# A two-layer graph attention kernel: scores issued in one run, the opening and the last row regrouped, and one product for q, k and v in odd groups

## The chip, the cores and the metric

The kernel runs on one core of one Trainium2 chip. The metric is device time in microseconds, the median of several runs. Everything is fp32, apart from the adjacency mask (bytes).

## The reference

The input is 128 graphs of 128 nodes with 512 features each, and a boolean adjacency mask per graph. Two layers follow each other. Each computes attention between the nodes of a graph, masked by the adjacency, projects the result back to 512 features, adds its own input, and normalises the rows.

```python
# layer 0: 4 heads of 64; layer 1: 8 heads of 64
q, k, v = x @ Wq, x @ Wk, x @ Wv
sim = where(adj, q @ k.T * 64**-0.5, -finfo.max)
x = layernorm(x + softmax(sim) @ v @ Wo + bo)
h = layernorm(x) * gamma + beta
q, k, v = split(h @ w_qkv.T)
scores = where(adj | eye, q @ k.T * 64**-0.5, -1e9)
x = layernorm(x + softmax(scores) @ v @ w_out.T + b_out)
```

## The kernel before

Two graphs make one group; there are 64 groups (0 to 63). The work is software-pipelined over groups, with the order of every engine's instructions written out by hand: there is no scheduler. `opening()` handles the first groups, `step(s)` runs for s = 2 to 63, then come `closing_a`, `closing_b` (twice) and `last`. In step s the kernel computes

- layer 0's q, k, v of group s (`product_0`), its scores and softmax for group s - 1 (part 0), and its attention output and projection for group s - 2 (`attend(s, 0)`, `out_product(0, s - 2, ...)`);
- layer 1's q, k, v of group s - 3 (`qk`, `v`), its scores and softmax for group s - 4 (parts 1 and 2, one graph each), and its attention output and projection for group s - 5 (`attend(s, 1, 2)`, `out_product(1, s - 5, ...)`).

Every large product is a 2x2 block product in seven partial products, numbered 1 to 7. The sums of inputs that they need are made on GpSimd (`sums`, `out_sums`), the sums of weights once in the opening (`weight_sums...`). Partial products accumulate in PSUM banks: "a" and "f" (and "a0" and "f0") are single banks, and "mm" is a ring of four. Partial products 1, 5 and 6 are copied out by ScalarE (tiles `e`, `ev`, `eqk`), 2, 3 and 7 are added to such a copy by VectorE, and 4 is copied by ScalarE.

`scores(s, part)` multiplies q by k of 64-row heads, `masked` moves the scores under the mask into the tile `sm` (VectorE, L585), `maxima` takes negated row maxima (VectorE, L591), `exps` are ScalarE's, `normalised` multiplies by the reciprocal sum on GpSimd (L609), `blocks` turns the probabilities by 32x32 transposes and a round trip through DRAM (`blocks_direct` turns them on TensorE instead, L651), and `attend` multiplies them by v. Part 0's and part 2's scores take two banks each of the ring; part 1's take "a0" and "f0". `attend` of part 0 writes to "a", of part 1 to "f", of part 2 to the ring.

Layer 1's q and k of a group take a round trip through DRAM as well: `taken_tokens` writes them out, `kq_arrive` (on SP's queue) fetches them into `KQ`, and `q_in_order` (ScalarE, L426) makes from them the tiles `qo` (one for each graph), which `scores` reads as the stationary operand. `norms` (ScalarE, L746) are put on the list `later` and issued by `flush()`. `addend` (GpSimd, L701) adds the bias to the rows, and `with_self` (VectorE, L564) adds the diagonal to the mask of layer 1.

The tile `qkv0` has four slots of 128 columns per graph and head pair: even groups use slots 1 to 3 (q, k, v), odd groups slots 0 to 2. So v of two groups can be alive while q and k share slots. In the odd groups the kernel before keeps q in slot 1, k in slot 2 and v in slot 0, so that a partial product is issued as two matmul shapes, 256 columns (q, k) and 128 columns (v), into one bank. Groups 0 to 2 (`PLAIN_0`) hold q and k features by tokens and are computed in pieces of 128 columns. An fp32 matmul appears in the trace as two records for each instruction.

The last group's projection is plain (`out_plain`): two halves of 256 columns for each graph, in one bank for each graph. `add_plain` adds a half to the rows and takes its statistics; `root_plain` and `norm_plain` finish a row.

Of the kernel before, what the change touches and what calls it, by code (L numbers as in the profile page):

```python
# [10 lines left out]
F32 = mybir.dt.float32  # L11
# [6 lines left out]
P = 128  # L18
# [9 lines left out]
def kernel(ctx: ExitStack, tc: tile.TileContext, x, adj, wq, wk, wv, wo, bo,  # L28
                            gamma, beta, w_qkv, w_out, b_out, out):
    nc = tc.nc  # L30
# [15 lines left out]
    ps_st = ctx.enter_context(tc.tile_pool(name="ps_st", bufs=1, space=PSUM))  # L46
# [97 lines left out]
    wo1 = const.tile([P, INNER[1] // P, E], F32, name="wo1")  # L144
# [50 lines left out]
    KH = KC // 2  # L195
# [33 lines left out]
    qkv0 = const.tile([P, G, 2, 4, P], F32, name="qkv0")  # L229
# [30 lines left out]

    PLAIN_0 = (0, 1, 2)

    def turn_qk0(g):

        if not 0 <= g < NG or g in PLAIN_0:
            return
        t = one.tile([P, 4, 2, 4, 32], F32, tag="turned", bufs=2, name=f"turnedqk_{g}")
        for i in range(2):
            nc.vector.transpose(t[:, :, i], qkv0.rearrange("p b h t (q j) -> p q t (b h) j", j=32)[:, :, 1 + i])
        SCR[0] = put(t.rearrange("p q t m j -> p q (t m j)"), f"scrqk_{g}")  # L270

    def arrive_qk0(g):
# [3 lines left out]

    def q0_in_order(g):
        if 0 <= g < NG and g not in PLAIN_0:
            nc.scalar.copy(qkv0.rearrange("p b h t (a j) -> p t (b h) a j", j=32)[:, 1],
                           RAW[0][:, :, 0].rearrange("p a m j -> p m a j"))  # L280

    def finish(g, half):
# [29 lines left out]
    def sums(l, g):  # L312
        if not 0 <= g < NG:
            return
        xs = XS[l, g] = one.tile([P, 4, KH, N], F32, tag=f"xs{l}", name=f"xs{l}_{g}")
        halves_sums(xs, XT[l, g].rearrange("p (h c) (b n) -> p b h c n", h=2, b=2))
# [10 lines left out]
    XS, ACC, EV = {}, {}, {}  # L327
# [119 lines left out]
    def product_0(g, *which, ts=(0, 1, 2)):  # L447

        if not 0 <= g < NG:
            return  # L450
        xT = XT[0, g].rearrange("p (h c) (b n) -> p b h c n", h=2, b=2)
        xs = XS[0, g]
        odd = g % 2
        for i in which:
            left = {1: xT[:, 0, 0], 2: xT[:, 0, 1], 3: xs[:, 3], 4: xT[:, 1, 1], 5: xs[:, 0],
                    6: xs[:, 1], 7: xs[:, 2]}[i]
            right = {1: w0[:, :KH, :, 0], 2: w0[:, KH:, :, 0], 3: w0[:, KH:, :, 1], 4: ws0[:, 2],
                     5: w0[:, :KH, :, 1], 6: ws0[:, 0], 7: ws0[:, 1]}[i]
            bank, first = INTO[i]
            first = first and ts in ((0, 1, 2), (1,))  # L460
            if first and bank == "c":
                ACC[0, bank] = mm_tile(f"c0_{g}")
            elif first:
                ACC[0, bank] = ps_st.tile([P, 512], F32, tag=f"{bank}0", name=f"{bank}0_{g}")
            acc = ACC[0, bank]
            parts = acc[:, :3 * P].rearrange("p (t n) -> p t n", n=P)
            if g in PLAIN_0:
                todo = [(parts[:, (t + odd) % 3], *((right[:, c, t], left[:, c]) if t < 2 else
                                                    (left[:, c], right[:, c, t])))
                        for t in ts for c in range(KH)]  # L470
            elif odd:
                todo = [(parts[:, lo:hi], left[:, c], right[:, c, t0:t1])
                        for lo, hi, t0, t1 in ((1, 3, 0, 2), (0, 1, 2, 3)) for c in range(KH)]
            else:
                todo = [(parts, left[:, c], right[:, c]) for c in range(KH)]
            for n, (o, lhsT, rhs) in enumerate(todo):
                nc.tensor.matmul(o, lhsT, rhs, start=first and n == 0, stop=n == len(todo) - 1,  # L477
                                 skip_group_check=True)
            if 2 not in ts:
                continue  # L480
            src = acc[:, :3 * P]

            def whole(b, h):
                return qkv0[:, b, h, 1 - odd:4 - odd].rearrange("p t n -> p (t n)")

            if i in (1, 5, 6):
                EV[0, i] = one.tile([P, 512], F32, tag=f"e{i}", name=f"e0_{i}_{g}")[:, :3 * P]
                nc.scalar.copy(EV[0, i], src)
            elif i == 4:
                nc.scalar.copy(whole(1, 0), src)  # L490
            else:
                b, h, e = {2: (0, 0, 1), 3: (0, 1, 6), 7: (1, 1, 5)}[i]
                nc.vector.tensor_add(whole(b, h), src, EV[0, e])


    def out_product(l, g, *which):
# [35 lines left out]
    def scores(s, *parts):  # L532

        made = {}
        for part in parts or PARTS:
            g = group_of(s, part)
            if g is None:
                continue
            if part == 1:
                ps = [ps_st.tile([P, 512], F32, tag=t, name=f"sc{part}_{g}_{t}") for t in ("a0", "f0")]  # L540
            else:
                ps = [mm_tile(f"sc{part}_{g}_{i}") for i in range(2)]
            ps = [x.rearrange("p (k n) -> p k n", n=N) for x in ps]
            if part == 0:
                for b in range(G):
                    for h in range(HEADS[0]):
                        r = slice((h % 2) * D, (h % 2 + 1) * D)
                        k_ = (qkv0[r, b, h // 2, 2].rearrange("p (a j) -> p a j", j=32) if g in PLAIN_0 else
                              RAW[0][r, :, 1, b * K0 + h // 2])
                        nc.tensor.matmul(ps[h % 2][:, b * K0 + h // 2, :].rearrange("p (a j) -> p a j", j=32),  # L550
                                         qkv0[r, b, h // 2, 1], k_, start=True, stop=True)
            else:
                b = part - 1
                for h in range(HEADS[1]):
                    r = slice((h % 2) * D, (h % 2 + 1) * D)
                    nc.tensor.matmul(ps[h % 2][:, h // 2, :].rearrange("p (a j) -> p a j", j=32),  # L556
                                     QO[g, b][r, h // 2], KQ[r, :, 0, b, h // 2], start=True, stop=True)
            made[part] = ps
        return made

    def with_self(g):

        if 0 <= g < NG:
            nc.vector.tensor_tensor(M[g], M[g], eye[:, None, :].to_broadcast([P, G, N]), op=ALU.max)  # L564
# [195 lines left out]
    def out_plain(g, b, *steps):  # L760

        n = E // 2
        if 0 in steps:
            ACC["op", b] = ps_st.tile([P, 512], F32, tag=("a0", "f0")[b], name=f"op_{b}")
        acc = ACC["op", b]
        for i in steps:
            h = slice(i * n, (i + 1) * n)
            for c in range(K1):
                nc.tensor.matmul(acc[:, h], AT[1, g][:, b, c], wo1[:, c, h], start=i == 0 and c == 0,
                                 stop=c == K1 - 1, skip_group_check=True)  # L770

    def add_plain(g, b, i):

        n = E // 2
        h = slice(i * n, (i + 1) * n)
        row = R[g][:, b, h]
        if i == 0:
            ST[b] = two.tile([P, 2, nc.vector.BN_STATS_DIM], F32, tag="st_last", name=f"st_last{b}")
        nc.vector.tensor_add(row, ACC["op", b][:, h], row)
        nc.vector.bn_stats(ST[b][:, i], row)  # L780

    def root_plain(b):
# [26 lines left out]
    def opening():  # L809
# [20 lines left out]
        made = scores(1)  # L830
# [16 lines left out]
        prepare(2)  # L847
        product_0(1, 4)
        transposed(2)
        sums(0, 2)  # L850

    def step(s):

        made = scores(s, 0)
        attend(s, 1)
        made.update(scores(s, 1, 2))
        if s > 3:
            sums(0, s)
            arrive(s - 3)
# [1 line left out]
        load_ahead(s + 1)  # L861
        load_rows(s - 1)
        masked(made, s, 0, 1, 2)
        attend(s, 0, 2)
        maxima(s, *((0,) if s == 4 else (0, 1)))
        if s == 3:
            turn(s - 3)
            arrive(s - 3)
        out_sums(0, s - 2)
        if s == 3:  # L870
            sums(0, s)
            with_self(s - 3)
        exps(s, 0, 0)
        product_0(s, 1)
        exps(s, 0, 1)
        out_product(0, s - 2, 1, 2, *(() if s == 2 else (5,)))
        maxima(s, *((1, 2) if s == 4 else (2,)))
        product_0(s, 2)
        if s == 2:
            out_product(0, s - 2, 5, 6)  # L880
        normalised(s, 0)
        out_product(0, s - 2, *(() if s == 2 else (6,)), 3)
        exps(s, 1, 0)
        stats(0, s - 2, 0)
        product_0(s, 6)
        exps(s, 1, 1)
        out_product(0, s - 2, 7)
        (blocks_direct if s == 2 else blocks)(s, 0)
        product_0(s, 5)
        out_product(0, s - 2, 4)  # L890
        normalised(s, 1)
        finish(s - 3, 0)
# [7 lines left out]
        blocks(s, 1)  # L900
        product_0(s, 3)
        if s == 3:
            weight_sums(w1qk, wsqk, 1)
        product_0(s, 4)
        transposed(s + 1)
# [36 lines left out]
        out_product(1, s - 5, 7, 3, 4)  # L942
        q0_in_order(s)
        q_in_order(s - 3)
        addend(0, s - 1)
        v(s - 3, 7)
        stats(1, s - 5, 0)
        v(s - 3, 3)
        stats(1, s - 5, 1)
        v(s - 3, 4)  # L950
        if s > 2:
            with_self(s - 2)
        if s == NG - 1:
            arrive(s - 2)
            addend(1, s - 4)
# [197 lines left out]
```

## Time and profile before

| what | value |
|---|---|
| median of 3 runs | 2761.13 us (2759.78 to 2761.82) |
| the profiled execution | 2759.77 us |
| its span, first to last instruction | 2758.0 us |
| mean granted TensorE clock | 0.999 |
| TensorE matmul busy | 2743.3 us, 15811 records |
| TensorE weight loads busy | 2032.5 us |
| VectorE busy | 2033.5 us |
| ScalarE busy | 1506.1 us |
| GpSimd busy | 1752.0 us |
| DMA moved | 562.73 MB, 204 GB/s in the mean |

In lines of the profile, PE is TensorE's matmul, PEld its weight load, DVE VectorE, ACT ScalarE, POOL GpSimd and SP the queue that issues the DMAs. A timeline line gives the start in us from the beginning of the span, the time in us, engine, line of the kernel and operation, what is written and read, the shape, and how many like records were merged; in brackets stands the engine's idle time before it, with what ended it. Ends of matmuls are modelled and overlap the next start, so distances between starts are the better measure.

### The profile page before, as it was taken

What the parts mean: (1) busy time and instruction counts of PE and PEld (TensorE: products, weight loads), DVE (VectorE), ACT (ScalarE), POOL (GpSimd) and SP (SyncE); (2) the same over time, 40 slices, a digit from 0 to 9 for tenths busy, and PEclk for the clock granted to TensorE, in tenths of its full rate; (3) what the DMA queues carried; (4) which work ended last, traced back from release to release, by engine and by line L of the source; (5) the groups of instructions that cost most, each with busy time, mean ns of one, the idle gap of its engine ahead of it and who ended that gap; (6) DMA issues with size and microseconds to landing.
All of it is one profiled execution on the core that took longest, in us unless ns stands there. A gap on an engine that the chain in (4) does not pass through costs nothing.

```text
span 2758.0 us, 49315 instructions
## 1 busy us (share of the span) xinstructions
PE 2743.3 (99%) x15811; PEld 2032.5 (74%) x15811; DVE 2033.5 (74%) x3671; ACT 1506.1 (55%) x4804; POOL 1752.0 (64%) x2311
## 2 busy tenths in 40 slices
PE   9999999999999999999999999999999999999998
PEld 8867767677776677776776767777767777677688
DVE  6777777777777777777777777777777777777765
ACT  3456465464564654645646546456465464564654
POOL 5565666666656666666566666665666666656664
PEclk9999999999999999999999999999999999999999
DMA  6567777777777777777777777777777777777652
GB/s 179 154 200 206 218 217 204 218 210 215 212 202 219 216 204 219 210 216 209 205 217 217 204 219 210 214 213 203 216 218 203 215 214 215 211 204 220 201 150 65
DMA packets 550290, 562.73 MB, mean 204 GB/s; under 512 B 55560, under 2 KB 468752, under 8 KB 550032
## 3 DMA queue, kind: packets, MB, share of 16 engines
q1 hardware_dynamic: 550032, 559.58, 71.5%
q8 instruction: 127, 2.08, 0.3%
q14 instruction: 131, 1.07, 0.1%
HBM read 300.95 MB, written 258.47 MB: 203 GB/s over the span
## 4 chain that ended last, share of the span: by engine, by line
PE 97%; DMA 1%; DVE 1%; issue 0%; SPq 0%; ACT 0%; POOL 0%; POOLq 0%; DVEq 0%; ACTq 0%
PE qka L361 16%; PE a L477 12%; PE oa L517 12%; PE va L361 8%; PE qkf L361 8%; PE av L679 7%; PE f L477 6%; PE of L517 6%; PE vf L361 4%; PE qkc L361 4%; PE oc L517 3%; PE c L477 3%; PE sc L550 2%; PE sc_a L556 2%; PE sc L556 2%; PE vc L361 2%
## 5 line engine op out<-in xcount | busy, mean ns | idle before, releaser
L600 ACT ACTIVATE sm<-sm,nmax 128x128 f32<-128x128 f32 x1536 | 594.8, 391 | 30.6 <-DVE nmax L591 27.9
L609 POOL TENSOR_TENSOR sm<-sm,rec 128x1024 f32<-128x1024 f32 x192 | 364.1, 1896 | 333.7 <-DVE rec L608 330.7
L701 POOL TENSOR_TENSOR r<-r,bias 128x1024 f32<-128x1024 f32 x128 | 301.5, 2356 | 130.9 <-ACT r L700 130.9
L521 DVE TENSOR_TENSOR r<-oa,r 128x256 f32<-128x256 f32 x508 | 211.1, 415 | 134.9 <-PE oa L517 129.4
L600 ACT ACTIVATION_READ_ACCUMULATOR sm<-sm,nmax 128x1 f32 x1536 | 291.4, 190 | 0.0
L371 ACT COPY ev<-va 128x256 f32<-128x256 f32 x128 | 47.6, 372 | 432.8 <-PE va L361 432.8
L627 DVE STREAM_TRANSPOSE turnedp<-sm 128x1024 f32<-128x1024 f32 x188 | 233.6, 1243 | 64.5 <-POOL sm L609 53.9
L720 POOL TENSOR_SCALAR ve<-mv 128x2 f32<-128x2 f32 x191 | 41.7, 218 | 371.4 <-DVE mv L713 360.9
L591 DVE TENSOR_REDUCE nmax<-sm 128x8 f32<-128x1024 f32 x192 | 226.6, 1206 | 0.3
L361 PE MATMUL qkf<-w,xs 128*128 128x512 f32 x472 | 221.8, 592 | 0.0
L361 PE MATMUL qka<-wsqk,xs 128*128 128x512 f32 x472 | 221.8, 592 | 0.0
L517 PE MATMUL of<-wo,so 128*128 128x256 f32 x760 | 205.9, 379 | 1.4 <-DVE r L521 1.0
L517 PE MATMUL oa<-wso,so 128*128 128x256 f32 x760 | 206.0, 380 | 0.4 <-DVE r L521 0.4
L324 POOL TENSOR_TENSOR xs<-xT 128x256 f32<-128x256 f32 x256 | 187.7, 733 | 22.4 <-DVE xT L118 18.6
L746 ACT ACTIVATE r<-r,shift,root 128x512 f32<-128x512 f32 x254 | 193.0, 809 | 2.5 <-POOL shift L735 2.5
L426 ACT ACTIVATE qo<-kq 128x512 f32<-128x512 f32 x118 | 67.9, 622 | 228.6 <-DMA kq<-scrkq 228.6
L324 POOL TENSOR_TENSOR so<-aT 128x256 f32<-128x256 f32 (+1 forms) x254 | 150.2, 591 | 52.1 <-ACT aT L682 44.6
L477 PE MATMUL f<-w,xs 128*128 128x128 f32 (+1 forms) x760 | 182.2, 376 | 0.2 <-DVE w L214 0.2
L477 PE MATMUL a<-ws,xs 128*128 128x128 f32 (+1 forms) x760 | 182.1, 375 | 0.0
L585 DVE COPY_PREDICATED sm<-m,sc 128x512 f32<-128x512 uint8 x256 | 172.4, 727 | 11.1 <-PE sc L550 2.2
L712 DVE BATCH_NORM_STATS2 st<-r 128x6 f32<-128x512 f32 x254 | 174.9, 689 | 2.3
L571 POOL MEMSET sm<- 128x1024 f32 x192 | 175.1, 952 | 1.4 <-DVE turnedp L627 1.4
(181 smaller groups left out, 6471.9 us busy)
## 6 DMA issues: line engine op xcount, KB each, us to landing
scrp<-turnedp SPq DMA_DIRECT2D x188, 512.0 KB, 3.6
pT<-scrp SPq DMA_DIRECT2D x752, 128.0 KB, 2.9
kq<-scrkq SPq DMA_DIRECT2D x236, 256.0 KB, 4.8
x<-in_x_dram SPq DMA_DIRECT2D x256, 128.0 KB, 4.0
r<-in_x_dram SPq DMA_DIRECT2D x64, 512.0 KB, 4.0
out_dram<-r SPq DMA_DIRECT2D x63, 512.0 KB, 3.6
scr<-turned SPq DMA_DIRECT2D x62, 512.0 KB, 6.7
kq<-scr SPq DMA_DIRECT2D x248, 128.0 KB, 2.8
```

The lines of the kernel that those rows point to most:

```text
L324: nc.gpsimd.tensor_tensor(o, a0, a1, op=op)
L361: nc.tensor.matmul(o, lhsT, rhs, start=first and m == 0, stop=m == len(todo) - 1, skip_group_check=True)
L477: nc.tensor.matmul(o, lhsT, rhs, start=first and n == 0, stop=n == len(todo) - 1, skip_group_check=True)
L517: nc.tensor.matmul(acc, left[:, c], right[:, c], start=first and c == 0, stop=c == hk - 1, skip_group_check=True)
L521: nc.vector.tensor_add(part, acc, part)
L591: nc.vector.tensor_reduce(NMAX[part], SM[part], AX.X, ALU.max, negate=True)
L600: nc.scalar.activation(sm[:, i, k, :], sm[:, i, k, :], AF.Exp, bias=nmax[:, i, k:k + 1], accum_out=total[:, i, k:k + 1])
L609: nc.gpsimd.tensor_tensor(SM[part], SM[part], rec[:, :, :, None].to_broadcast([P, 2, K1, N]), op=ALU.mult)
L627: nc.vector.transpose(t.rearrange("p q (h r) -> p q h r", r=32), SM.pop(part).rearrange("p i k (q r) -> p q (i k) r", r=32))
L679: nc.tensor.matmul(pm[i * D:(i + 1) * D, at, :].rearrange("p (a r) -> p a r", r=32), v, pT[:, :, i * K1 + at, :], start=True, stop=True)
L701: nc.gpsimd.tensor_tensor(R[g], R[g], (bias0, bias1)[l][:, None, :].to_broadcast([P, G, E]), op=ALU.add)
L746: nc.scalar.activation(R[g][:, b], R[g][:, b], AF.Identity, bias=shift[:, b:b + 1], scale=root[:, b:b + 1])
```

## The change

The change has four parts; `closing_a`, `closing_b` and the order of `last` keep as they are.

- `step` issues the scores of all three parts in one run, and then all three parts of `attend`, in the order 0, 1, 2. Before, part 1's `attend` stood between the scores of part 0 and those of parts 1 and 2.
- `product_0` of odd groups issues one matmul of 384 columns for each half of the contraction instead of one of 256 and one of 128. The bank then holds q, k, v in this order in all groups. For odd groups the evictions write the three runs backwards, so that v stays in slot 0, k in slot 1 and q in slot 2; `QK0` tells the readers where q and k are.
- In `opening` and steps 2 to 4: the input sums of group 2 move from the end of the opening into step 2, behind the output sums; part 0's exps move as a whole behind the first `product_0`; in step 4 part 2's maximum moves behind part 1's first exps; in step 2 `blocks_direct` moves behind one more product; in step 3 an `addend` moves ahead of a block of weight sums, and `with_self` of group 0 moves to the end of the step.
- `out_plain` puts each half into a bank of its own, four in all.

```diff
+    QK0 = ((1, 2), (2, 1))
...
-            nc.vector.transpose(t[:, :, i], qkv0.rearrange("p b h t (q j) -> p q t (b h) j", j=32)[:, :, 1 + i])
+            nc.vector.transpose(t[:, :, i], qkv0.rearrange("p b h t (q j) -> p q t (b h) j", j=32)[:, :, QK0[g % 2][i]])
...
-            nc.scalar.copy(qkv0.rearrange("p b h t (a j) -> p t (b h) a j", j=32)[:, 1],
+            nc.scalar.copy(qkv0.rearrange("p b h t (a j) -> p t (b h) a j", j=32)[:, QK0[g % 2][0]],
...
-                todo = [(parts[:, (t + odd) % 3], *((right[:, c, t], left[:, c]) if t < 2 else
+                todo = [(parts[:, t], *((right[:, c, t], left[:, c]) if t < 2 else
...
-            elif odd:
-                todo = [(parts[:, lo:hi], left[:, c], right[:, c, t0:t1])
-                        for lo, hi, t0, t1 in ((1, 3, 0, 2), (0, 1, 2, 3)) for c in range(KH)]
             else:
                 todo = [(parts, left[:, c], right[:, c]) for c in range(KH)]
...
             def whole(b, h):
-                return qkv0[:, b, h, 1 - odd:4 - odd].rearrange("p t n -> p (t n)")
+                return qkv0[:, b, h, 2::-1] if odd else qkv0[:, b, h, 1:4]
...
-                nc.scalar.copy(EV[0, i], src)
+                nc.scalar.copy(EV[0, i], acc[:, :3 * P])
             elif i == 4:
-                nc.scalar.copy(whole(1, 0), src)
+                nc.scalar.copy(whole(1, 0), parts)
             else:
                 b, h, e = {2: (0, 0, 1), 3: (0, 1, 6), 7: (1, 1, 5)}[i]
-                nc.vector.tensor_add(whole(b, h), src, EV[0, e])
+                nc.vector.tensor_add(whole(b, h), parts, EV[0, e].rearrange("p (t n) -> p t n", n=P))
...
+                        q_at, k_at = QK0[g % 2]
-                        k_ = (qkv0[r, b, h // 2, 2].rearrange("p (a j) -> p a j", j=32) if g in PLAIN_0 else
+                        k_ = (qkv0[r, b, h // 2, k_at].rearrange("p (a j) -> p a j", j=32) if g in PLAIN_0 else
                               RAW[0][r, :, 1, b * K0 + h // 2])
...
-                                         qkv0[r, b, h // 2, 1], k_, start=True, stop=True)
+                                         qkv0[r, b, h // 2, q_at], k_, start=True, stop=True)
...
     def out_plain(g, b, *steps):
         n = E // 2
-        if 0 in steps:
-            ACC["op", b] = ps_st.tile([P, 512], F32, tag=("a0", "f0")[b], name=f"op_{b}")
-        acc = ACC["op", b]
         for i in steps:
-            h = slice(i * n, (i + 1) * n)
+            acc = ACC["op", b, i] = ps_st.tile([P, 512], F32, tag=(("a0", "a"), ("f0", "f"))[b][i], name=f"op_{b}{i}")
             for c in range(K1):
-                nc.tensor.matmul(acc[:, h], AT[1, g][:, b, c], wo1[:, c, h], start=i == 0 and c == 0,
+                nc.tensor.matmul(acc[:, :n], AT[1, g][:, b, c], wo1[:, c, i * n:(i + 1) * n], start=c == 0,
                                  stop=c == K1 - 1, skip_group_check=True)
...
-        nc.vector.tensor_add(row, ACC["op", b][:, h], row)
+        nc.vector.tensor_add(row, ACC["op", b, i][:, :n], row)
...
         transposed(2)
-        sums(0, 2)
 
     def step(s):
-        made = scores(s, 0)
-        attend(s, 1)
-        made.update(scores(s, 1, 2))
+        made = scores(s)
...
-        attend(s, 0, 2)
+        attend(s)
         maxima(s, *((0,) if s == 4 else (0, 1)))
...
         out_sums(0, s - 2)
-        if s == 3:
+        if s in (2, 3):
             sums(0, s)
-            with_self(s - 3)
-        exps(s, 0, 0)
+        if s > 4:
+            exps(s, 0, 0)
         product_0(s, 1)
-        exps(s, 0, 1)
+        exps(s, 0, *((0, 1) if s < 5 else (1,)))
         out_product(0, s - 2, 1, 2, *(() if s == 2 else (5,)))
-        maxima(s, *((1, 2) if s == 4 else (2,)))
+        maxima(s, 1 if s == 4 else 2)
...
         exps(s, 1, 0)
+        if s == 4:
+            maxima(s, 2)
...
-        (blocks_direct if s == 2 else blocks)(s, 0)
+        if s > 2:
+            blocks(s, 0)
         product_0(s, 5)
+        if s == 2:
+            blocks_direct(s, 0)
...
         product_0(s, 3)
         if s == 3:
+            addend(0, s - 1)
             weight_sums(w1qk, wsqk, 1)
...
-        addend(0, s - 1)
+        if s != 3:
+            addend(0, s - 1)
...
-        if s > 2:
-            with_self(s - 2)
+        for g in {2: (), 3: (0, 1)}.get(s, (s - 2,)):
+            with_self(g)
```

More of the change, by code (lines that the diff above doesn't have):

```diff
@@ L480, in product_0 @@
                 continue
-            src = acc[:, :3 * P]
             def whole(b, h):
-                return qkv0[:, b, h, 1 - odd:4 - odd].rearrange("p t n -> p (t n)")
+                return qkv0[:, b, h, 2::-1] if odd else qkv0[:, b, h, 1:4]
             if i in (1, 5, 6):
                 EV[0, i] = one.tile([P, 512], F32, tag=f"e{i}", name=f"e0_{i}_{g}")[:, :3 * P]
-                nc.scalar.copy(EV[0, i], src)
+                nc.scalar.copy(EV[0, i], acc[:, :3 * P])
             elif i == 4:
-                nc.scalar.copy(whole(1, 0), src)
+                nc.scalar.copy(whole(1, 0), parts)
             else:
                 b, h, e = {2: (0, 0, 1), 3: (0, 1, 6), 7: (1, 1, 5)}[i]
-                nc.vector.tensor_add(whole(b, h), src, EV[0, e])
+                nc.vector.tensor_add(whole(b, h), parts, EV[0, e].rearrange("p (t n) -> p t n", n=P))
     def out_product(l, g, *which):
```

## The prediction

> **What bounds the kernel now.** I read the page first (busy shares, then the chain that ended last), then a window over the steady part, then TensorE's timeline of one step.
>
> ```profile
> PE 2743.3 (99%) x15811; PEld 2032.5 (74%) x15811; DVE 2033.5 (74%) x3671; ACT 1506.1 (55%) x4804; POOL 1752.0 (64%) x2311
> PE 97%; DMA 1%; DVE 1%; issue 0%; SPq 0%; ACT 0%; POOL 0%; POOLq 0%; DVEq 0%; ACTq 0%
> 130.00:2588.00 2458.00, 2458.00 (x13659) 1782.16 (x13656) 1831.57 (x3302) 1359.82 (x4345) 1578.72 (x2080) 1.00 0.75 212
> ```
>
> From 130 to 2588 us the matrix engine has no idle time, at a full clock. Only what shortens TensorE's own stream, or makes it wait, moves the end. A busy PE is not a PE at its peak, so I take the distance between **starts** in the timeline, not durations. One step (it starts at its first score matmul, L550) has a switch of matmul kind three times in its head:
>
> ```profile
> 1315.74 1.16 PE L550 MATMUL sc<-rawqk,qkv 64*128 64x128 f32 x16
> 1316.83 1.09 PE L679 MATMUL av<-pT,v 128*64 128x128 f32 x16
> 1317.86 0.37 PE L556 MATMUL sc_a<-kq,qo 64*128 64x128 f32 x1
> ...
> 1318.85 1.06 PE L556 MATMUL sc<-kq,qo 64*128 64x128 f32 x16
> 1319.84 1.09 PE L679 MATMUL av<-pT,qkv 128*64 128x128 f32 x16
> 1320.77 1.04 PE L679 MATMUL av<-pT,v 128*64 128x128 f32 x16
> 1321.74 1.57 PE L477 MATMUL a<-w,xT 128*128 128x256 f32 x8
> ```
>
> Step 4 has no attend of part 1 yet, so its three score groups already stand in one run:
>
> ```profile
> 92.35 1.16 PE L550 MATMUL sc<-rawqk,qkv 64*128 64x128 f32 x16
> ...
> 95.22 1.09 PE L679 MATMUL av<-pT,qkv 128*64 128x128 f32 x16
> 96.25 1.56 PE L477 MATMUL a<-w,xT 128*128 128x384 f32 x4
> ```
>
> And the products of layer 0, in an odd step (two shapes, 8 records) and in an even one (4 records):
>
> ```profile
> 1331.41 1.47 PE L477 MATMUL f<-w,xs 128*128 128x256 f32 x8
> 1332.72 1.47 PE L477 MATMUL a<-ws,xT 128*128 128x256 f32 x8
> ...
> 106.45 1.45 PE L477 MATMUL f<-w,xs 128*128 128x384 f32 x4
> 107.74 1.45 PE L477 MATMUL a<-ws,xT 128*128 128x384 f32 x4
> ```
>
> **What the Trainium skill says.** "TensorEngine Tiling (Array Packing)", Key Properties: changing the tiling mode, not just the tile, drains TensorE. The trace agrees: scores use 64 rows (64*128), attend 64 columns (128*64), products the whole array. Pairs of records follow each other every 0.112 us in a score run and every 0.109 us in an attend run; a pair at a switch takes 0.20 to 0.21 us and the next one is late again, while sc to sc_a and av to av cost nothing extra. "TensorE: Matmul & The Clock Gate", LDWEIGHTS (loading the stationary operand): a load costs columns/1.2, thus 107 ns for 128 columns (an estimate from the page). A 128x128 matmul record starts its successor 111 ns later, against 106.7 ns for 128 columns within wider records (322.5 for 384 minus 215.8 for 256): it lies at that floor. "SBUF — State Buffer", Who interferes with whom: VectorE and GpSimd share a port pair under an exclusive lock. The trace agrees in the opening: a VectorE weight sum (L214, at 81.09 us) took 2.57 us beside a GpSimd add, its like just before 0.42.
>
> **The change part by part.**
>
> 1. Scores in one run, steps 5 to 63 (59 steps). Before, head to first product: 1321.74 - 1315.74 = 6.00 us. After: scores in one run 95.22 - 92.35 = 2.87; then av, av, av. The two av runs that already follow each other take 1321.74 - 1319.84 = 1.90; another 8 pairs at 0.109 add 0.87. Sum 5.64 to 5.65. Saved 0.354 us (from the unrounded starts) x 59 = **-20.9 us**. No matmul is removed; one return to scores (0.20) and one more entry into attend (0.15) are.
>
> 2. Odd groups' q, k, v in one product. 31 odd groups (3 to 63), 7 products each. An odd product takes 1.307 to 1.310 us (four records at 215.8 and four at 111 ns), an even one 1.290. Over a step it is 0.13: odd steps last 42.49 us from scores to scores, even ones 42.35. 31 x 0.13 = **-4.0 us**. It removes 31 x 7 x 4 = 868 matmul records and as many weight loads. The evictions change only their order of writing (three runs of 128, backwards); no row of before shows a backward write. Forward they take 0.55 us on VectorE and 0.46 on ScalarE. If backward cost half more, three VectorE adds would add 0.8 us in a step in which VectorE is busy 1831.57/2458 = 75%; that hides in its 10 us of idle time, otherwise it would delay TensorE by at most that. I take 0. The changed index of the transposes and of ScalarE's q copy moves the same bytes.
>
> 3. A new wait. sc_a now starts about 1.0 us after the step's start instead of 2.1, and needs qo of half 0, which ScalarE makes when the kq DMAs land:
>
> ```profile
> 1315.24 1.15 ACT L426 ACTIVATE qo<-kq 128x512 f32<-128x512 f32 x2 [3.69 <-DMA kq<-scrkq]
> ```
>
> Half 0 is done at 1315.87, 0.13 after the step's start. Over the steps with such rows its median is 0.25 after the start, with a scatter of -0.6 to +2.02. In 8 (steps 7, 9, 17, 38, 44, 54, 61, 63) it comes later than 0.92, which leaves 0.08 for the semaphore; the excess sums to **+3.1 us**. Before, 2.1 us covered all: the waits of TensorE show this one once, 0.9 us, in the closing. Everything on TensorE queues behind sc_a: the second half's scores, the three attends, product 1. The kq DMAs are issued from SP after the qk products of the step before, whose distance to the step's end doesn't change, so I keep this distribution; half a microsecond of general delay makes 9.3. Bounds: +1 to +9.
>
> Part 1's eviction on ScalarE now stands behind the norms (done near +4.3 in the step) and lands near +5.6; the first to need its bank is the of matmul at +8. sc_a's banks come free at the last r add, 2.06 us before the step's start. VectorE gets its last scores earlier and is done with masking near +5.2 instead of 5.97, while the first product moves only to 5.65: no new wait. SP issues nothing for attend; its order is unchanged there.
>
> 4. Opening, steps 2 to 4. Waits of TensorE there, from starts against the record's own spacing: 0.53 and 0.98 (of at 43.91 and 45.95), 0.47 (pt at 48.70), 0.35 (of at 65.08), 0.60 (qka at 84.32), 0.55 (oa at 102.93), together 3.5 us.
>
> ```profile
> 45.95 0.67 PE L517 MATMUL of<-wo,so 128*128 128x256 f32 x2 [0.81 <-DVE r L521]
> 102.93 0.67 PE L517 MATMUL oa<-wso,so 128*128 128x256 f32 x2 [0.38 <-DVE r L521]
> ```
>
> Each edit meets one: sums(0, 2) go behind the out sums on POOL (so was ready 2 to 3 us late); the exps go behind ScalarE's e copy, on which a VectorE eviction and then the r adds waited; the transposes by TensorE go one product (1.3 us) later; with_self leaves the head of step 3; one maximum (1.2 us) leaves the queue ahead of r in step 4; the addend (2.5 us on POOL) moves away from weight sums, the 2.57 us one among them. It then lies beside transposes and other weight sums, and may delay qk there. No DMA moves. I take **-3.0**; bounds -3.5 and +1.
>
> 5. Last row. Four banks instead of two: VectorE's add of half 0 no longer waits for the whole row.
>
> ```profile
> 2751.11 0.42 DVE L779 TENSOR_TENSOR r<-op,r 128x256 f32<-128x256 f32 x1 [1.47 <-PE op L769]
> 2752.36 0.42 DVE L779 TENSOR_TENSOR r<-op,r 128x256 f32<-128x256 f32 x1
> ```
>
> Half 0 is then added near 2749.5, the first row's norm fits before 2751.1, and the last add starts at 2751.11 instead of 2752.36: **-1.25**; bounds 0 and -1.4. The two further banks were evicted before 2744.
>
> Sum: -20.9 - 4.0 + 3.1 - 3.0 - 1.25 = -26.0. The profiled execution took 2759.77 (span 2758.0 and 1.77 around it): 2733.7. The median of the runs, 2761.13, lies 1.36 higher, and I give the time against it: **2735.0**, 0.9% below. About 0.2%, 5.5 us, is what a measurement of this kernel can tell from no change.
>
> **Rivals.** (a) *The drain stays*: the cost belongs to each block's entry, not to the mode. Then part 1 gives nothing: 2735 + 21 = 2756, faster by 0.19%, no change. Against it stand the blocks of like kind that follow each other at full pace. Chance 0.02. (b) *qo becomes the bound*, the slower side: the kq round trip through DRAM ends later in every step, because the DMA queues (75% busy) or SP's order shift. Shifting the measured arrivals by 1.05 us makes the waits 28 us and eats all gains; at 1.5 us they are 52, and the time is 2735 + 49 = 2784. For it: ScalarE waits 3.7 us for this DMA per step, so nothing but the DMA sets it. Against: what feeds it is not moved. Chance 0.04. (c) *The opening gives nothing or a microsecond back, and late kq transfers come often*: 2735 + 4 + 6 = 2745, still faster. Chance 0.12, within the forecast's sign. The forecast proper has 0.82.
>
> The range adds the bounds: best -20.9 - 4.3 + 1 - 3.5 - 1.4 = -29, thus 2732, less 2 for scatter between runs; worst with +9 and no gain in the opening -17, 2744. I give 2730 to 2743. Faster 0.94, same 0.02, slower 0.04.
>
> **What would show it.** Right: 48 av records in one run after 48 score records, steps of 42.0 us, odd and even alike; no 128x128 or 128x256 form of layer 0's products in odd groups after 1; about 14943 matmul records; waits "sc_a from ACT qo" in some eight steps, 2 to 5 us in all; no wait for r at 45 and 103 us; the last VectorE chain about 1.2 us shorter. Wrong: sc_a waiting in most steps, VectorE evictions above 0.7 us in odd steps, odd steps still 0.13 longer, or TensorE waiting for masked scores ahead of product 1.

## The result, and the profile after

The changed kernel takes 2736.12 us (median of 4 runs, 2734.58 to 2737.01), beside 2760.73 for the kernel before (4 runs): a ratio of 0.991, with a 95% interval of 0.9893 to 0.9927. The forecast was 2735.0. The profiled execution took 2737.01 us, its span 2735.2: 22.8 less than the span of before.

From the page of the changed kernel, the busy line, and from a window over its steady part the row of busy times:

```profile
PE 2720.4 (99%) x14943; PEld 1933.5 (71%) x14943; DVE 2027.1 (74%) x3671; ACT 1503.3 (55%) x4804; POOL 1750.5 (64%) x2311
130.00:2567.00 2437.00, 2435.13 (x12818) 1687.42 (x12812) 1828.22 (x3300) 1356.93 (x4345) 1576.64 (x2080) 1.00 0.75 213
```

14943 matmul records are 868 fewer, as counted. TensorE still sets the end, but is no longer without a gap: 1.87 us of idle time have come into the window, where there was none.

TensorE's timeline of the head of step 32 in the changed kernel (columns: start, time, engine, line, operation, output and inputs, shape, count; layer 1's scores, between the first two rows, are left out):

```profile
1262.71 1.16 PE L548 MATMUL sc<-rawqk,qkv 64*128 64x128 f32 x16
...
1265.59 1.09 PE L677 MATMUL av<-pT,qkv 128*64 128x128 f32 x16
1266.51 1.92 PE L677 MATMUL av<-pT,v 128*64 128x128 f32 x32
1268.36 1.56 PE L476 MATMUL a<-w,xT 128*128 128x384 f32 x4
```

All 48 score records come first, then 48 av records, with no gap at a seam between blocks of like kind. The head of a step, from its first score to its first product, takes 1268.36 - 1262.71 = 5.65 us, where the kernel before took 6.00. The distance from one step's first score to the next's is 42.00 us in odd and even steps alike (before: 42.49 and 42.35).

Where the 22.8 us of the span went, from the starts of the steps in both profiles: the start of step 1 came 1.5 later (the weights' first DMAs landed later; in the twelve profiles of this study it lies anywhere from 22.1 to 23.9 us); step 1 to step 5 took 102.6 instead of 105.8 (-3.2; the two belong together, as the run with the opening's edits alone shows below, and make -1.7); the 58 steps from step 5 to step 63 took 2440.8 instead of 2460.4 (-19.6); step 63 47.2 instead of 48.3 (-1.1); from step 64's scores to the last matmul 115.2 instead of 114.4 (+0.8, of which 0.5 is a wait for ScalarE's xT that the profile of before does not have); the tail behind the last matmul 5.67 instead of 6.90 (-1.2). The profile of before fell on the fastest of its four runs and that of the changed kernel on the slowest of its four, so the spans differ by less than the medians (24.6).

The new wait is there too. The waits of TensorE, and step 26 in TensorE's and ScalarE's timelines:

```profile
PE sc_a L554 <- ACT qo L428: 1.9, 4, 0.9
1008.70 1.16 PE L548 MATMUL sc<-rawqk,qkv 64*128 64x128 f32 x16
1010.78 0.37 PE L554 MATMUL sc_a<-kq,qo 64*128 64x128 f32 x1 [0.92 <-ACT qo L428]
1010.10 1.15 ACT L428 ACTIVATE qo<-kq 128x512 f32<-128x512 f32 x2 [5.58 <-DMA kq<-scrkq]
```

ScalarE had been idle for 5.58 us until the kq DMAs landed; half 0 of qo (half of the 1.15) was done 2.03 us after the step's first score, and sc_a started 0.05 after that, at 2.08 instead of 1.0. The wait list counts 1.9 us in four gaps; measured on the starts, nine steps lost 4.3 in their heads. Steps 5 to 63 are 4.7 longer than their median in all: the other 0.4 lies almost wholly at the end of step 7, where the last partial product of layer 1's v waits for VectorE's copy of v.

### The profile page after: what moved, and what is told of

The parts are those of the page before. It is cut to its first block, busy times and chain, and to the rows that moved or that the text cites. A ratio compares the mean times of both kernels' runs of the same rounds, so it can differ in the third digit from the quotient of the medians.

```text
span 2735.2 us, 47645 instructions
## 1 busy us (share of the span) xinstructions
PE 2720.4 (99%) x14943; PEld 1933.5 (71%) x14943; DVE 2027.1 (74%) x3671; ACT 1503.3 (55%) x4804; POOL 1750.5 (64%) x2311
## 3 DMA queue, kind: packets, MB, share of 16 engines
q14 instruction: 130, 1.06, 0.1%
## 4 chain that ended last, share of the span: by engine, by line
PE 96%; DMA 2%; SPq 1%; ACT 0%; issue 0%; DVE 0%; POOL 0%; POOLq 0%; ACTq 0%; DVEq 0%
PE qka L363 16%; PE a L476 12%; PE oa L514 11%; PE qkf L363 8%; PE va L363 8%; PE av L677 6%; PE f L476 6%; PE of L514 6%; PE qkc L363 4%; PE vf L363 4%; PE c L476 3%; PE oc L514 3%; PE sc L548 2%; PE sc L554 2%; PE vc L363 2%; PE sc_a L554 2%
## 5 line engine op out<-in xcount | busy, mean ns | idle before, releaser
L476 PE MATMUL f<-w,xs 128*128 128x384 f32 (+1 forms) x512 | 181.1, 476 | 0.2 <-DVE w L214 0.2
L476 PE MATMUL a<-ws,xs 128*128 128x384 f32 (+1 forms) x512 | 181.0, 476 | 0.0
L514 PEld LDWEIGHTS oa<-wso,so 128*128 128x128 f32 x760 | 143.7, 190 | 45.7 <-issue 0.7
```

Of the source, the lines that this page charges most:

```text
L514: nc.tensor.matmul(acc, left[:, c], right[:, c], start=first and c == 0, stop=c == hk - 1, skip_group_check=True)
```

## The experiments

**Each part alone.** Four kernels, each the kernel before with one part of the change. Scores in one run:

```diff
-        made = scores(s, 0)
-        attend(s, 1)
-        made.update(scores(s, 1, 2))
+        made = scores(s)
...
-        attend(s, 0, 2)
+        attend(s)
```

> The kernel before, with the scores of all parts in one run and the three attends behind them; nothing else is changed. My theory (each change of matmul kind costs 0.15 to 0.20 us, two of them go in each of 59 steps): 59 x 0.354 = 20.9 us less, and 3 to 5 us come back in waits of sc_a for qo, so 2743 to 2745 us, the head of a step at 5.65 us and steps of 42.14 (odd) and 42.00 us (even). Rival (the cost belongs to every block's entry): heads stay at 6.0 us, and the time is that of before or up to 5 us more.

It took 2743.22 us (ratio 0.9935, 0.9922 to 0.9947), thus 18.0 less. Its step 33:

```profile
1308.85 1.16 PE L550 MATMUL sc<-rawqk,qkv 64*128 64x128 f32 x16
...
1314.50 1.57 PE L477 MATMUL a<-w,xT 128*128 128x256 f32 x8
```

The head is 5.65 us, the steps 42.14 (odd) and 42.00 (even), and 4.8 us come back above these medians in the steps where qo is late: from step 5 to step 63, 58 x 0.349 = 20.2, less 4.8, leaves 15.5 of the 18.0; another 1.4 go in step 63 (46.9 instead of 48.3), of which 0.35 is its own head and the rest a wait for qo that the kernel before has there. These are my theory's numbers; the rival's head of 6.0 is not seen.

One product in odd groups:

```diff
-            elif odd:
-                todo = [(parts[:, lo:hi], left[:, c], right[:, c, t0:t1])
-                        for lo, hi, t0, t1 in ((1, 3, 0, 2), (0, 1, 2, 3)) for c in range(KH)]
...
-                return qkv0[:, b, h, 1 - odd:4 - odd].rearrange("p t n -> p (t n)")
+                return qkv0[:, b, h, 2::-1] if odd else qkv0[:, b, h, 1:4]
```

> The kernel before, with one product of 384 columns in the odd groups and evictions written backwards; nothing else is changed. My theory: 4.0 us less, about 2757 us; odd steps as long as even ones (42.35 us), head at 6.0 us, evictions on VectorE still 0.55 us. Rival (the backward write costs time, or the narrow records were hidden under other work): evictions of 0.6 us or more in odd steps, and a time within 1 us of before.

It took 2754.87 us (0.9978, 0.9969 to 0.9987), thus 6.3 less, more than the 4.0. In TensorE's timeline of an odd step the products now follow each other at 1.29 us:

```profile
1329.56 1.45 PE L476 MATMUL f<-w,xs 128*128 128x384 f32 x4
1330.85 1.45 PE L476 MATMUL a<-ws,xT 128*128 128x384 f32 x4
```

Odd steps fell from 42.49 to 42.35, and the time from step 5 to step 63 from 2460.43 to 2456.47 together: 4.0, as expected. The span is shorter by another 1.2 in step 63 (47.1 instead of 48.3), where here too the one wait of the kernel before is missing. Why it is gone stays open. The last microsecond that the runs show beyond the profiles is no gain: the profiled execution of before, 2759.77 us, was 1.4 faster than the median of its runs here, 2761.22. In odd steps the evictions written backwards take what they took forwards: 547 ns in the median on VectorE in both, 463 on ScalarE against 457.

The changed order of the opening and of steps 2 to 4, and the last row's four banks:

> The kernel before, with the changed order of the opening and of steps 2 to 4 only. My theory: the start of step 1 to the start of step 5 takes 102.6 us instead of 105.8, so about 3.2 us less in all, and nothing after that. Rival (the waits are only pushed on, or are those of the weights' DMAs at the start): that stretch is shorter by less than 1 us, or what it gains is lost by step 6.

> The kernel before, with four banks for the last row's halves only. My theory: from the last matmul's end to the span's end 5.67 us instead of 6.9, so 1.2 us less. Rival (the row's store ends last anyway): below 0.4 us.

The opening's edits alone gave 2759.44 us (0.9993, 0.9985 to 1.0002), the last row's 2759.42 (0.9994, 0.9986 to 1.0002). Neither interval excludes no change, so the runs alone do not decide; the profiles show where the time goes. Step 1 to step 5 took 102.75 us in the first, nearly as in the changed kernel, and 105.80 before: 3.05 less, and after it 0.4 come back (steps 5 to 63: 2460.8 against 2460.4), nearly all of it in step 7 by the wait for VectorE's copy of v. But its step 1 began 1.2 later, at the weights' DMAs, and a late start shortens this stretch by itself. The runs with the last row alone and with the scores alone have the old opening; their step 1 also began late, at 23.55 and 23.48, and step 1 to step 5 took 104.68 and 104.60. The largest old wait, at 45.95 in the profile of before (0.81), is small there; from TensorE's timeline of the run with the last row alone:

```profile
46.42 0.67 PE L517 MATMUL of<-wo,so 128*128 128x256 f32 x2 [0.19 <-POOL so L324]
```

So I count from the beginning of the span instead. The four kernels with the old opening start step 5 between 127.93 and 128.23 us, wherever their step 1 began; the opening's edits alone start it at 126.12. Up to there they are worth 1.8 us, before the 0.4 that come back. The rival is thus right in part: the other 1.2 of the 3.05 us hang on when the weights' DMAs land.

In the second, the tail is 5.66 us instead of 6.91; its last add on VectorE starts 0.04 after the last matmul's end at 2751.72:

```profile
2751.76 0.42 DVE L776 TENSOR_TENSOR r<-op,r 128x256 f32<-128x256 f32 x1 [0.39 <-PE op L766]
```

The four parts alone sum to 18.0 + 6.3 + 1.8 + 1.8 = 27.9 us, together they gave 25. With intervals of 2 to 3.5 us either way on each, that difference is no finding; the profiles' spans give 16.39 + 4.98 + 1.06 + 0.59 = 23.0, against 22.8 together.

**A change of kind, or a block's entry?** The changed kernel, with scores and attend in turn:

```diff
-        made = scores(s)
+        made = scores(s, 0)
+        attend(s, 0)
+        made.update(scores(s, 1))
+        attend(s, 1)
+        made.update(scores(s, 2))
...
-        attend(s)
+        attend(s, 2)
```

> The changed kernel, but with scores and attend in turn: scores of part 0, attend 0, scores 1, attend 1, scores 2, attend 2. The same blocks and the same matmuls, with two returns to scores and two entries into attend more than in the changed kernel. My theory (a change of kind costs): the head of a step goes from 5.65 to 5.65 + 2 x 0.354 = 6.36 us, over 59 steps 42 us more, less the 4 us of waits for qo that the later sc_a no longer meets: about 2774 us, slower than the kernel before by 0.5%. Rival (the cost belongs to each block's entry, whatever stands before it, or to the first wait on a bank): the count of blocks is the same, so 2732 to 2738 us.

It took 2814.87 us (1.0197, 1.0182 to 1.0212): slower, as my theory has it, but by far more. The miss is a wait that I had not seen; from its waits of TensorE, and its timeline:

```profile
PE av L677 <- ACT v L386: 26.6, 35, 1.8
563.12 1.09 PE L677 MATMUL av<-pT,qkv 128*64 128x128 f32 x16 [1.25 <-ACT v L386]
```

attend 0 writes to bank "a", which ScalarE empties (the copy of v) only behind q_in_order, which waits for the kq DMAs. Put behind the first scores, attend 0 needs this bank 1.1 us into the step. Heads range from 6.347 to 8.18 us; those without a wait are 6.347, and the excess over that sums to 30.3 us from step 5 to step 63. Behind the head, the rest of a step takes 36.56 us in the median instead of 36.35, another 12.6 us in all, whose cause I did not trace. So the run told of kind and bank together, and did not part the theories cleanly.

The second try takes the waits away. It starts from the kernel with the queries fetched first (below), in which qo and the copy of v are early, and puts attend 1 first:

```diff
-        made = scores(s)
+        made = scores(s, 0)
+        attend(s, 1)
+        made.update(scores(s, 1))
+        attend(s, 0)
+        made.update(scores(s, 2))
...
-        attend(s)
+        attend(s, 2)
```

> The kernel with the queries fetched first, with scores and attend in turn once more, but so that no new wait is met: scores of part 0, attend 1 (as in the kernel before, its bank is freed by VectorE), scores 1, attend 0, scores 2, attend 2. My theory (a change of kind costs 0.15 or 0.20 us): head 5.65 + 0.71 = 6.36 us, steps of 42.71, 59 x 0.71 = 42 us more than with the queries first alone, about 2773 us. Rival (a block's entry costs whatever stands before it, and the first run of turns was slow through its waits alone): no waits now, so 2731 to 2735 us.

It took 2775.93 us (1.0055, 1.0039 to 1.007), 44.8 more than its base. TensorE's timeline of step 33 (the sc_a records stand singly in it and are left out but for the first):

```profile
1322.11 1.16 PE L550 MATMUL sc<-rawqk,qkv 64*128 64x128 f32 x16
1323.20 1.09 PE L679 MATMUL av<-pT,v 128*64 128x128 f32 x16
1324.22 0.37 PE L556 MATMUL sc_a<-kq,qo 64*128 64x128 f32 x1
...
1328.45 1.56 PE L478 MATMUL a<-w,xT 128*128 128x384 f32 x4
```

No row of these heads waits for anything, and every head is 6.347 or 6.348 us: 0.699 more than 5.649 (40.5 of the 42.9 us by which steps 5 to 63 are longer), for two returns to scores and two entries into attend more. The other 2.4 us are 0.34 in each of seven steps (every eighth, 11 to 59), 11 to 13 us into the step and so behind the head; their cause is open. The same blocks with the same matmuls cost 0.35 us less per pair of turns when like stands beside like. The rival (each block pays an entry) is out.

**Is the narrow record the cost of the odd product?** The same base, with two shapes in all groups, unrotated:

```diff
-                todo = [(parts, left[:, c], right[:, c]) for c in range(KH)]
+                todo = [(parts[:, lo:hi], left[:, c], right[:, c, lo:hi])
+                        for lo, hi in ((0, 2), (2, 3)) for c in range(KH)]
```

> The kernel with the queries fetched first, with layer 0's q, k, v in two matmuls of 256 and 128 columns in the even groups as well as in the odd ones, all into the same places as now. My theory (the narrow record sits at the floor of its weight load): each product is 0.0175 to 0.02 us longer, all steps last 42.13 to 42.14 us, about 61 x 0.13 = 8 us more than with the queries first alone: 2739 us. Rival (the odd groups' cost came from their rotated places in the bank): steps stay at 42.00, and 2731 us.

It took 2739.66 us (0.9926, 0.9914 to 0.9939), 8.5 more than its base. TensorE's timeline of step 33:

```profile
1325.73 1.47 PE L479 MATMUL f<-w,xs 128*128 128x256 f32 x8
1327.04 1.47 PE L479 MATMUL a<-ws,xT 128*128 128x256 f32 x8
```

A product takes 1.31 us instead of 1.29, and a step 42.142 us instead of 42.002, even ones included: 8.1 us from step 5 to step 63. So two records cost more than one, and the places in the bank have nothing to do with it.

That the weight load sets the 111 ns of the narrow record is not shown. The starts follow each other by 429.1, 322.5 and 215.8 ns for 512, 384 and 256 columns: 106.7 for each 128 columns, and 2.4 left for every record whatever its width. On that line a record of 128 columns would take 109.1; it takes 111. Of the 4.3 ns that a pair of records costs more than a single one, 2.4 is thus what any further record pays, and 1.9 the narrow one's own. The profile's weight-load records do not settle it: they overlap the matmuls and each other, and those of 128 columns on the whole array last 190 ns in the median.

**The wait for qo.** First made worse: the changed kernel with qo's first half made twice.

```diff
-            for b in range(G):
+            for b in (0, *range(G)):
...
```

> The changed kernel, with the ScalarE instruction that makes qo of the first graph given twice, so that each half of qo is done 0.62 us later (the result is the same). My theory (a step loses the time by which qo is later than 0.775 us after its first score matmul, by the arrivals in the changed kernel's profile): with all arrivals 0.62 later the waits sum to about 18 us instead of 4.5, so about 2750 us. Rival (arrivals wait for TensorE in some way, so that they move with it, or ScalarE has room before the DMA lands): within 3 us of the changed kernel.

It took 2752.03 us (0.9967, 0.9954 to 0.9979), 16 more than the changed kernel; expected were 14. The waits of TensorE now show it sixteen times instead of four:

```profile
PE sc_a L554 <- ACT qo L428: 9.5, 16, 1.8
```

So arrivals do not move with TensorE, and 0.62 us of delay at this place cost 16 us of the end. Then made better, by splitting the fetch of layer 1's keys and queries:

```diff
-            fetch(KQ.rearrange("p a w b c j -> p a (w b c j)"), SCRQ.pop(g).rearrange("p q w b x -> p q (w b x)"))
+            scr = SCRQ.pop(g)
+            for i in (1, 0):
+                fetch(KQ[:, :, i].rearrange("p a b c j -> p a (b c j)"), scr[:, :, i].rearrange("p q b x -> p q (b x)"))
```

> The changed kernel, with the fetch of layer 1's keys and queries split: the four DMAs of the queries first, then four of the keys. My theory: qo no longer waits for the keys' last transposes to come back, and is done 1 to 2 us earlier; the keys themselves, which now land last, need no ScalarE work, and are in time in most steps. The waits of sc_a shrink from 4.5 to 1 to 3 us, so 2733 to 2735 us. Rival (four more DMA issues of 0.43 us on SP push the keys, and the probabilities' fetch behind them, past the scores): the waits grow, 2738 us or more.

It took **2731.15 us** (0.9892, 0.9877 to 0.9907), 4.7 less than the changed kernel beside it, and is the fastest kernel of the study. Its rows of the DMA issues, of ScalarE's timeline and of the busy times in the window:

```profile
kq<-scrkq SPq DMA_DIRECT2D x472, 128.0 KB, 3.1
1298.42 1.15 ACT L430 ACTIVATE qo<-kq 128x512 f32<-128x512 f32 x2
130.00:2562.00 2432.00, 2432.00 (x12819) 1686.26 (x12815) 1828.10 (x3298) 1360.88 (x4347) 1576.61 (x2080) 1.00 0.74 214
```

Twice as many DMAs of half the size, and qo's first half is done 3.5 us before the step's first score in the median, instead of 0.3 after it; the latest is 1.7 before. Steps 5 to 63 take 2436.09 us, 58 times 42.002 without a remainder, and TensorE has no idle time in the window again. The keys land last, but no score waited for them: no row of the waits names them.

Not all of the 4.7 us is the wait for qo. The spans of the two profiles differ by 4.4: 2.5 are the waits for qo in the heads, 0.4 those of step 63, 0.35 the wait at the end of step 7, and 1.1 lie in the closing, 0.8 of them a wait for ScalarE's xT. The two other kernels with the queries first have that last wait again (0.4 and 1.6 us), so about 3.3 us are the fetch's own.

The changed kernel as it is, beside these:

> The changed kernel as it is, for comparison on the same chip: 2735 to 2738 us, 0.991 of before, with waits of sc_a for qo in some eight steps, in other steps than in its first profile, 3 to 6 us in all.

It took 2735.84 us (0.9908, 0.9893 to 0.9923). Its profile has six steps with qo later than 0.92 (28, 33, 45, 59, 60, 61), and its heads lost 2.5 us instead of 4.3. I had expected other steps than in the first profile; all six were late there too. In these two executions, lateness thus belongs in the main to the program's pattern of transfers. Its size does scatter: step 26, which lost 1.26 us in the first, lost 0.09 in the second.

## Why the prediction was right, point by point

The whole came out at -24.6 us (medians) and -22.8 (spans) where -26.0 was forecast. The parts are those of the sum; of the five, the opening was sized too large, and the wait for qo came near with a wrong bound:

| step of the prediction | forecast, us | measured, us | from |
|---|---|---|---|
| scores in one run | -20.9 | -20.6 | heads 5.998 and 5.649, 59 steps |
| one product in odd groups | -4.0 | -4.0 | steps 5 to 63 with this part alone; 42.49 to 42.35 |
| waits of sc_a for qo | +3.1 | +4.3, +2.5 | heads over their median, two profiles |
| opening | -3.0 | -1.8 | beginning of the span to step 5, with this part alone |
| last row | -1.25 | -1.2 | last matmul to the span's end |

Scores: the sum of blocks, with step 4 as the pattern, held to 0.005 us per step. That a change of kind costs this time is shown by the turns; that it is a drain of the engine, as the prediction reads it, is in keeping with them and not shown apart. The later eviction of part 1, the masking and the banks that the prediction went through are in no wait of the profile, as it said. Two waits that it did not foresee came in elsewhere: 0.35 us at the end of step 7, which the opening's edits alone also show, and 0.5 and 0.8 us for xT in the closing.

Odd groups: right in size, and the two-shape run shows that the second, narrow record is the cost. The reason given for it, that this record lies at the floor of its weight load, is not shown: the 107 ns that it takes for a load are also what 128 columns take within the wider records, and over half of the cost is what any further record pays. The backward writes cost nothing on VectorE and 6 ns an eviction on ScalarE.

The wait for qo was the right mechanism with a term sized too small. The prediction let a step lose what qo was later than 0.92, because it added only the semaphore. Measured, a step loses what it is later than 0.77: in step 26, qo was done at 2.03 and the first product was late by 1.26; in step 60, 1.07 and 0.29. In every late step of both profiles and of the kernel with qo made later, the difference is 0.769 to 0.773. The rest beyond the semaphore grows in the first records after the wait: in step 26 sc_a started 1.09 us late, and a few records on, 0.3 us after it, the stream was 1.26 late, as if the start of a score run were paid a second time. With this bound the forecast's own arrivals would have given 4.4 instead of its 3.1. The late steps are not those of the kernel before (of its eight only 61 is among them): that the sum came near is in part luck, and it was 4.3 us in one profile and 2.5 in the other.

Opening: this term was too large, 3.0 where 1.8 came. It counted the waits of one profile, in which step 1 began early; where it began late, those of step 2 were smaller without any edit. And new waits took the place of some, so that its own sign, no wait for r at 45 and 103 us, did not come. The changed kernel still waits at 46.1 us (0.44), and in step 4 a later product waits in place of the old one; from its timelines of VectorE and TensorE:

```profile
100.83 1.21 DVE L589 TENSOR_REDUCE nmax<-sm 128x8 f32<-128x1024 f32 x1
103.22 0.70 PE L514 MATMUL oa<-wso,aT 128*128 128x256 f32 x2 [0.73 <-DVE r L518]
```

The maximum that was moved behind the exps stands ahead of the statistics and of the r add, which only then frees the bank. The addend beside other weight sums, which the prediction feared for, delayed nothing on TensorE.

The range, said to add the bounds, leaves two of them out: with +1 for the opening and 0 for the last row its slow end would have been 2746, not 2743. The measured time lies well inside either.

## What to carry to other kernels

When the matrix engine has no gaps, look at its starts. In this kernel a return from attend's 64 columns to the scores' 64 rows and back cost 0.35 us, and blocks of like kind cost nothing at their seams, so matmuls of one kind are worth putting in runs. Moving work forward in such a stream uses up the cover of what it reads; take the arrival times of those inputs from the trace, step by step, and sum what is late, with the restart of the run included. Compare stretches of two profiles from a point that both reach alike: a stretch that begins late can be shorter for that alone. What is late by a DMA may be cured by splitting the transfer, so that the half that still needs work on another engine comes first.

## What the runs showed that I had not expected

The split fetch, queries first, did far better than one in four DMAs of 256 KB, though each DMA costs SP about 0.43 us to issue: qo is done 3.8 us earlier, where 1 to 2 were expected. The size alone is little of it: from the first issue to the last landing, eight DMAs took 6.85 us in the median and four 7.4. Another 0.8 us is an earlier first issue, whose reason is open; the rest is that qo no longer waits for the keys' half of the bytes.
